# A graph attention kernel with a guarded second pass: TensorE's last branch is marked as likely taken as well

## The chip, the cores and the metric

The kernel runs on one core of a Trainium2 chip. The metric is the device time of one launch in microseconds (us). Before the change it is 612.53 us, the median of three runs (611.76, 612.53 and 612.70). One further execution was profiled.

## What is computed

Two graph attention layers (8 heads of 768 columns, then 1 head) over 512 nodes and 16,896 edges, a residual sum and a layer norm over the rows:

```python
def gat_layer(x, W, a_s, a_d, b, edge_index, concat):
    h = (x @ W).reshape(n, H, C)
    alpha_s = jnp.einsum('nhc,hc->nh', h, a_s)
    alpha_d = jnp.einsum('nhc,hc->nh', h, a_d)
    e = jax.nn.leaky_relu(alpha_s[src] + alpha_d[dst], NEG_SLOPE)
    m = jax.ops.segment_max(e, dst, num_segments=n)
    e = jnp.exp(e - m[dst])
    alpha = e / (jax.ops.segment_sum(e, dst, num_segments=n)[dst] + EPS)
    out = jax.ops.segment_sum(h[src] * alpha[:, :, None], dst, num_segments=n)
    return out.reshape(n, H * C) + b

h = jax.nn.elu(gat_layer(x, W1, ..., concat=True))
x = layernorm(x + gat_layer(h, W2, ..., concat=True))
```

## The kernel before

The edges become a dense 512x512 matrix of counts, so that each layer is a row of matrix products in float32, 128 nodes a tile. Heads are taken one after another. For each, TensorE (PE) projects x with that head's columns of W1, weighs the rows with the softmax over edges, and multiplies the result with that head's rows of W2; the sums over the heads collect in the tile `h2`. Products are split by Strassen's scheme (`P1` to `P7`, and `P0` to `P14` in thirds), which is why VectorE (DVE) adds and subtracts tiles all the time. ScalarE (ACT) takes exponentials and copies, GpSimd (POOL) issues weight loads, and SyncE (SP) issues most other transfers.

The order of the work is written by hand: strings of names such as `END`, which `run` (L724) calls one after another, so that each engine gets its instructions in the order of the names. `END` holds the last head's second half, the second layer, and the layer norm of four tiles of 128 rows. Its names that matter here:

- `f.P7.1`, `f.P5.1`, `f.P4.1`, `f.P2.1`, `f.P3.1a`, `f.P3.1b`: the last products of TensorE (L1348 and L1371);
- `all`, `inv`: mean, root and reciprocal of a tile's rows; `whole2`, `whole0`, `whole3`: the scaled rows go out in one transfer of 384 KB each, issued by SP (L1462);
- `left1`, `right1`: the last tile goes out in two halves of 192 KB, one issued by SP and one by ACT (L1455);
- `hint`: the mark that this change adds to (L1486).

A fast way of counting edges holds only where no two nodes share too many of them. So the whole pass is written twice. The first pass, with the fast count, leaves a number (`again`) which says whether it held, and behind it stands a branch on all five engines (L33): where `again` is not zero, the general pass runs, and otherwise the program goes on at a short block that stands behind the general pass. With these inputs `again` is zero, and the general pass is jumped over. Behind that block all engines meet, and the program ends.

The mark `LikelyTaken` for the branch `again` is written in `hint` for ACT, DVE and SP, near the end of `END`. As the program is built, the instruction that carries it (BRANCH_PREFETCH_HINT) doesn't stand there: on each of the three engines it is the first instruction of the first pass.

## Time and profile before

| what | value |
|---|---|
| median of the runs | 612.53 us (611.76 to 612.70) |
| the profiled execution's own time | 611.53 us |
| its span, first to last instruction | 609.7 us |
| around the span | 1.83 us |
| TensorE busy | 600.4 us, 98% of the span |
| VectorE, ScalarE, GpSimd busy | 517.9, 305.4, 100.6 us |
| bytes moved by DMA | 114.24 MB |
| granted TensorE clock | 0.997 |

Times in the views count from the span's first instruction. An engine's own name (PE for products, PEld for weight loads) stands for work of the engine, and a name that ends in q (PEldq, SPq) for its sequencer, which waits, branches and issues transfers. The page's busy times leave the sequencers out, so a branch is seen only in the view of its source line. The DMA view counts packets, bytes and, as a share of what 16 DMA engines could give in that window, the time that the packets took. Queues of the kind "instruction" bring the engines' own code.

### The profile page before, as it was taken

To read this page: it belongs to the slowest core of one execution; us is meant where nothing else is said; L and a number is where in the kernel's file an instruction comes from. 1 tells how busy PE (TensorE), PEld (TensorE's weight loads), DVE (VectorE), ACT (ScalarE), POOL (GpSimd) and SP (SyncE) were. 2 spreads that over 40 slices of the span, in tenths; PEclk is the share of its full clock that TensorE was granted. 3 is DMA by queue.
4 is the path that set the end of the run, shared out by engine and by line. 5 is a ranking of instruction groups with operands and counts; after the bars stand their busy time and mean duration, and the time that the engine had idled before them with its cause. 6 is when DMAs were issued, how large, how long until landed. Compare 5 with 4: busy or idle time off the path is not lost.

```text
span 609.7 us, 8353 instructions
## 1 busy us (share of the span) xinstructions
PE 600.4 (98%) x2812; PEld 492.3 (81%) x2812; DVE 517.9 (85%) x1027; ACT 305.4 (50%) x563; POOL 100.6 (17%) x140
## 2 busy tenths in 40 slices
PE   9999999999999999999999999999999999999994
PEld 5665685788888888888888888888888888887863
DVE  7979968779997789878897789977897789989984
ACT  3128776624745166442746066532755147744743
POOL 2210103040301302022300303012210304022001
PEclk9999999999999999999999999999999999999998
DMA  8973898794947959395955939297883949593203
GB/s 302 314 169 90 251 273 200 217 287 78 346 70 237 212 179 244 51 336 81 330 110 174 268 127 291 47 300 133 273 167 113 294 92 261 104 238 56 53 17 109
DMA packets 97343, 114.24 MB, mean 187 GB/s; under 512 B 42966, under 2 KB 78222, under 8 KB 96398
## 3 DMA queue, kind: packets, MB, share of 16 engines
q1 hardware_dynamic: 75230, 89.26, 45.9%
q0 software_dynamic: 21632, 23.79, 24.6%
q10 hardware_dynamic: 432, 0.59, 0.3%
q8 instruction: 24, 0.39, 0.3%
q14 instruction: 25, 0.20, 0.1%
HBM read 99.05 MB, written 2.90 MB: 167 GB/s over the span
## 4 chain that ended last, share of the span: by engine, by line
PE 98%; DVE 0%; ACT 0%; issue 0%; DVEq 0%
PE mm L552 22%; PE mm L472 18%; PE mm L986 17%; PE mm L413 12%; PE tr L552 5%; PE bc L986 4%; PE tr L472 4%; PE bc L472 4%; PE tr L986 3%; PE bc L552 3%; PE mm L1348 2%; PE mm L663 1%; PE bc L792 1%; PE tr L413 1%; PE bc L271 1%; PE bc L1348 0%
## 5 line engine op out<-in xcount | busy, mean ns | idle before, releaser
L560 DVE TENSOR_TENSOR h<-h,mm 128x512 f32<-128x512 f32 x74 | 50.5, 683 | 8.9 <-PE mm L552 8.1
L478 ACT ACTIVATE hs<-mm 128x512 f32<-128x512 f32 x26 | 15.5, 597 | 80.6 <-PE mm L472 79.9
L187 POOL DMA_DIRECT2D w2t<-in_L_gnn_W_dram x21 | 28.3, 1662 | 165.9 <-PE mm L472 84.0
L480 DVE TENSOR_TENSOR hs<-hs,mm 128x512 f32<-128x512 f32 x38 | 26.1, 687 | 27.0 <-PE mm L472 19.9
L986 PE MATMUL mm<-PT,hs 128*128 128x256 f32 x192 | 46.6, 380 | 0.0
L552 PE MATMUL mm<-w1r,gT 128*128 128x256 f32 x192 | 44.2, 380 | 0.0
L915 ACT ACTIVATE q<-q,rden 128x512 f32<-128x512 f32 x28 | 20.2, 720 | 42.7 <-DVE rden L899 42.5
L923 ACT COPY PT<-zr 128x1024 uint16<-128x1024 uint16 x35 | 40.4, 1158 | 2.2 <-DMA zr<-pS 1.2
L187 POOL DMA_DIRECT2D w2r<-in_L_gnn_W_dram x14 | 18.3, 1310 | 139.4 <-DVE gT L1038 77.3
L552 PEld LDWEIGHTS mm<-w1r,gT 128*128 128x128 f32 x192 | 36.4, 190 | 5.2 <-DVE gT L589 0.3
L986 PEld LDWEIGHTS mm<-PT,hs 128*128 128x128 f32 x192 | 36.2, 190 | 5.2 <-ACT u L997 0.2
L703 ACT ACTIVATE q<-q,nmax 128x512 f32<-128x512 f32 x36 | 26.0, 722 | 25.9 <-DVE nmax L700 25.9
L472 PE MATMUL mm<-w2r,gT 128*128 128x256 f32 x144 | 33.7, 379 | 0.0
L422 DVE SCALAR_TENSOR_TENSOR scr<-hs,a_s 128x768 bf16<-128x768 f32 x32 | 30.6, 955 | 0.7
L422 DVE SCALAR_TENSOR_TENSOR scr<-hs,a_d 128x768 bf16<-128x768 f32 x32 | 30.5, 952 | 0.3
L472 PEld LDWEIGHTS mm<-w2r,gT 128*128 128x128 f32 x144 | 27.3, 190 | 3.8 <-issue 0.2
L552 PE MATMUL mm<-w1t,gS 128*128 128x256 f32 x128 | 30.2, 379 | 0.0
L472 PE MATMUL mm<-w2r,xT 128*128 128x256 f32 x128 | 29.9, 379 | 0.0
L986 PE MATMUL mm<-pS,gS 128*128 128x256 f32 x120 | 29.3, 379 | 0.0
L918 ACT COPY pS<-q 128x1024 uint16<-128x1024 uint16 x27 | 28.1, 1045 | 0.7
L472 PEld LDWEIGHTS mm<-w2r,xT 128*128 128x128 f32 x128 | 24.3, 190 | 3.3
L552 PEld LDWEIGHTS mm<-w1t,gS 128*128 128x128 f32 x128 | 24.3, 190 | 3.3
(393 smaller groups left out, 1493.2 us busy)
## 6 DMA issues: line engine op xcount, KB each, us to landing
w2r<-in_L_gnn_W_dram SPq DMA_DIRECT2D x48, 384.0 KB
w1r<-in_L_gnn_W_dram SPq DMA_DIRECT2D x43, 384.0 KB
gT<-xd SPq DMA_DIRECT2D x6, 1280.0 KB
w2t<-in_L_gnn_W_dram SPq DMA_DIRECT2D x21, 256.0 KB
w2t<-in_L_gnn_W_dram POOLq DMA_DIRECT2D x21, 256.0 KB, 9.3
w1t<-in_L_gnn_W_dram SPq DMA_DIRECT2D x18, 256.0 KB
w1t<-in_L_gnn_W_dram POOLq DMA_DIRECT2D x18, 256.0 KB, 5.1
w2r<-in_L_gnn_W_dram POOLq DMA_DIRECT2D x14, 256.0 KB, 8.7
```

The source lines that it names most:

```text
L187: return lambda: nc.gpsimd.dma_start(o, part(k, n), accum_op=add)
L413: nc.tensor.matmul(ps[:, :HALF], A_[p][:, k, i * P:(i + 1) * P], B_[p][:, k, :], start=start and k == 0, stop=k == HK - 1, skip_group_chec ...
L422: return [lambda al=al, a=a, sign=sign: nc.vector.scalar_tensor_tensor(scr, HS[h][:, t, :], sign, a, op0=ALU.mult, op1=ALU.mult, accum_out ...
L472: nc.tensor.matmul(bank[chain][:, i * TH:(i + 1) * TH], A_[p][:, k, i * P:(i + 1) * P], B_[p][:, k, :], start=first and i == k == 0, stop= ...
L480: nc.vector.tensor_tensor(out(o), out(o), ps, op=how)
L552: nc.tensor.matmul(bank[chain][:, i * TH:(i + 1) * TH], A_[p][:, k, i * P:(i + 1) * P], B_[p][:, k, :], start=first and i == k == 0, stop= ...
L560: nc.vector.tensor_tensor(out(o), out(o), ps, op=how)
L703: nc.scalar.activation(q, q, AF.Exp, bias=nmax, scale=-1.0, accum_out=dens[t])
L915: nc.scalar.activation(q, q, AF.Copy, scale=rden)
L918: nc.scalar.copy(apart.rearrange("p (h n) -> p h n", h=2), q.bitcast(U16).rearrange("p (n h) -> p h n", h=2))
L923: copy(PT.rearrange("p s n -> p (s n)").bitcast(U16).rearrange("p (s n h) -> p s n h", s=NT, h=2)[:, :, t * P:(t + 1) * P, :], parted.pop( ...
L986: nc.tensor.matmul(st[bank][:, :HN], A_[p][:, k, c * P:(c + 1) * P], B_[p][:, k, :], start=start and k == 0, stop=k == 1, skip_group_check ...
```

## The change

`hint` keeps its three engines. A second step, `hintT`, writes the same mark for TensorE, and the name stands in `END` ahead of the last six calls that give TensorE work (twelve matmul statements).

```diff
-        f.fork1 f.P7.0 a3 c3 f.P6.1 zw0 f.P4.0 y22.0 sq2 sF0 f.P3.0 zu1 bn2L sA1 all2 f.P7.1 bn0L bn0R inv2 whole2 all0 f.P5.1
+        f.fork1 f.P7.0 a3 c3 f.P6.1 zw0 f.P4.0 y22.0 sq2 sF0 f.P3.0 zu1 bn2L sA1 all2 hintT f.P7.1 bn0L bn0R inv2 whole2 all0 f.P5.1
...
+    def hint_tensor():
+        if not general:
+            tc.mark_branch_hint_location("again", "LikelyTaken", [mybir.EngineType.PE])
+    ops["hintT"] = hint_tensor
```

What stands on TensorE at the start of the program, as a difference (a row with + is of the changed kernel; `zeros` is a tile that the first, empty products read; L1514 and L1519 are one and the same line of the two files):

```order
-L1514 UNCONDITIONAL_BRANCH
+L1519 UNCONDITIONAL_BRANCH
+L1519 BRANCH_PREFETCH_HINT
 L271 LDWEIGHTS zeros
 L271 MATMUL bc<-zeros 128x512
```

The one added instruction stands here, ahead of TensorE's first weight load, not where `END` names it.

What stands on TensorE in the changed kernel from the place where `END` has `hintT` to the branch (`xT`, `h` and `pS`, `PT` are the second layer's two factors, `mm`, `tr` and `bc` banks of sums):

```order
L1348 MATMUL mm_95<-h_633,PT 128x384 x2
L1348 MATMUL tr<-xT,pS 128x384 x2
L1348 MATMUL mm_95<-xT,PT 128x384 x2
L1348 MATMUL bc<-h_633,PT 128x384 x2
L1371 MATMUL tr<-h_633,pS 128x192 x4
L33 COMPARE_AND_BRANCH
```

These are the rows of before, word for word; nothing was added or moved here. The other four engines have the same instructions in the same order as before.

## The prediction

> **What bounds the kernel now.** I read the page first, for the engine that fills the span, then the last part of the chain that ended last, then the two source lines that hold the branch and the end of the program, and last the DMA view of the final microseconds, in ever narrower windows. The page:

> ```profile
> span 609.7 us, 8353 instructions
> PE 600.4 (98%) x2812; PEld 492.3 (81%) x2812; DVE 517.9 (85%) x1027; ACT 305.4 (50%) x563; POOL 100.6 (17%) x140
> PE 98%; DVE 0%; ACT 0%; issue 0%; DVEq 0%
> ```

> TensorE is busy for 98% of the span and is 98% of the chain. So a stall of TensorE ahead of its last product would lengthen the time by its full length, and only what comes behind that product is open to a change at the branch. The end of the chain, from the same view cut to the last 27 us (start, length, engine and line):

> ```profile
> 600.42 1.31 PE tr L1371 x8
> ...
> 602.69 0.30 ACT rstd L1435
> ...
> 603.41 0.67 ACT hs L1448
> ```

> TensorE's last product ends at 600.42 + 1.31 = 601.73, and the last computation of any engine at 603.41 + 0.67 = 604.08. The span goes on to 609.7: 5.6 us in which nobody computes. The branch (L33), by engine, with duration in ns (least, middle, most) and the first and last start:

> ```profile
> L33 SPq EVENT_SEMAPHORE  x8: 17/17/17, 604.9 to 607.9; - x8
> ...
> L33 PEldq COMPARE_BRANCH  x1: 3982/3982/3982, 599.3 to 599.3; - x1
> L33 POOLq COMPARE_BRANCH  x1: 45/45/45, 601.2 to 601.2; - x1
> L33 DVEq COMPARE_BRANCH  x1: 89/89/89, 603.2 to 603.2; - x1
> L33 PEldq EVENT_SEMAPHORE  x1: 51/51/51, 603.3 to 603.3; - x1
> ...
> L33 SPq COMPARE_BRANCH  x1: 73/73/73, 604.4 to 604.4; - x1
> L33 ACTq COMPARE_BRANCH  x1: 68/68/68, 604.5 to 604.5; - x1
> ```

> The reader is to see one number: 3982 ns on TensorE, against 68 to 89 ns on the three engines that carry the mark. TensorE's sequencer runs ahead of its products: it branches at 599.3, while products run until 601.73, and goes on at 603.3. The end of the program, from the line that holds it:

> ```profile
> L1514 SPq DRAIN  x3: 7/7/13, 608.8 to 609.1; - x3
> L1514 PEldq DRAIN  x2: 8/8/8, 603.5 to 609.1; - x2
> ...
> L1514 PEldq EVENT_SEMAPHORE  x2: 51/51/51, 609.0 to 609.6; - x2
> L1514 ACTq BRANCH_PREFETCH_HINT  x1: 50/50/50, 0.7 to 0.7; - x1
> L1514 SPq BRANCH_PREFETCH_HINT  x1: 51/51/51, 0.7 to 0.7; - x1
> L1514 DVEq BRANCH_PREFETCH_HINT  x1: 51/51/51, 0.8 to 0.8; - x1
> ```

> TensorE has drained at 603.5 and then waits until 609.0 for the meeting of all engines. SP comes there last: it passes eight semaphores, the last at 607.9, a dozen more behind them, and drains at 608.8. What SP waits for are the output transfers. So **the end is set by the landing of the last output, not by any branch**, and TensorE's long branch has 608.8 - 603.5 = 5.3 us to spare.

> **The change, part by part.** It adds one instruction to TensorE, the mark, at the program's start, and moves none; no queue is issued to at another place.

> The mark itself: 50 or 51 ns by the three rows above. Its neighbours on TensorE:

> ```profile
> L1505 PEldq EVENT_SEMAPHORE  x1: 51/51/51, 0.7 to 0.7; - x1
> ...
> 0.95 0.27 DVE L266 MEMSET zeros<- 128x256 uint32 x1 [0.95 <-PEq L1505]
> ...
> 1.27 0.13 PEld L271 LDWEIGHTS <-zeros 128*128 128x128 bf16 x2 [1.27 <-DVE zeros L266]
> ```

> The sequencer passes the first meeting at 0.7 and its first weight load waits until 1.27 for a tile that VectorE fills from 0.95 on. 0.05 us lie inside these 0.5 us: I take **nothing**, and 0.05 us if the cover is gone.

> The branch: by the three marked engines it should fall from 3982 ns to some 70 or 90. TensorE's sequencer would go on at about 599.4, wait for its products (601.73), drain near 602 in place of 603.5, and wait for the meeting all the same. The 3.9 us lie wholly in the 5.3 us of slack: **nothing** by itself. What is late next is what was late before, SP.

> The code packets: this is the only way to the end that I find. Two queues bring code, by the page in packets of 16 KB (0.39 MB in 24) and of 8 KB; behind them the two windows of the DMA view in which q8 moves something near the end, 600.2 to 600.4 and 604.0 to 604.2:

> ```profile
> q8 instruction: 24, 0.39, 0.3%
> q14 instruction: 25, 0.20, 0.1%
> ...
> q8 instruction: 1, 0.02, 44.6%
> ...
> q8 instruction: 1, 0.02, 39.9%
> ```

> I read q8 as TensorE's: one packet starts about 1 us behind its branch (599.3), the next when it has gone on (603.3). The first took 44.6% of 16 engines times 0.2 us = 1.43 us of one engine, the second 39.9% x 16 x 0.2 = 1.28 us. The second falls into the last wave of output transfers, issued here:

> ```profile
> 603.99 0.33 SPq L1455 DMA_DIRECT2D out_dram<-hs  x1
> 604.11 0.36 ACTq L1455 DMA_DIRECT2D out_dram<-hs  x1
> ```

> A DMA engine that spends 1.28 us on code is that much late with its sixteenth of the output. Is one engine late? Three more windows, 606.2 to 607.6, 607.1 to 607.6, and 607.135 to 607.6; q10 carries ACT's half tile, 144 packets in all by the first row (window 602 to 610), so 9 an engine:

> ```profile
> q10 hardware_dynamic: 144, 0.20, 7.1%
> ...
> DMA packets 50, 0.07 MB, mean 49 GB/s; under 512 B 7, under 2 KB 48, under 8 KB 50
> ...
> q10 hardware_dynamic: 27, 0.04, 7.1%
> q1 hardware_dynamic: 23, 0.03, 6.7%
> ...
> DMA packets 9, 0.01 MB, mean 18 GB/s; under 512 B 3, under 2 KB 9, under 8 KB 9
> ...
> DMA  3000030000300003000030000030000000000000
> DMA packets 7, 0.01 MB, mean 20 GB/s; under 512 B 1, under 2 KB 7, under 8 KB 7
> ...
> q10 hardware_dynamic: 7, 0.01, 5.4%
> ```

> Behind 606.2 there are 27 packets of q10 left: three engines with 9 each, while thirteen are done. Behind 607.1 nine are left, three of them small (an engine's closing one), behind 607.135 seven with one small: two of the three late engines close between 607.1 and 607.135. The row of digits shows what remains: packets at equal steps, about 60 ns apart (five steps in 26 slices of 11.6 ns), one engine alone. It is late by 5.4% x 16 x 0.465 = **0.40 us** against the other two, and its last packet leaves at 607.5; SP passes its last semaphore 0.4 us later, at 607.9. I take the engine that brought the 16 KB as that last one: 1.28 us of code is the largest disturbance in this stretch.

> [...] Then the two engines that are late already set the end, 0.40 us sooner. This term isn't shown by itself, so its bounds: 0, if the last engine is late for another reason or the fetch lands in the wave again; 1.28 us, the whole packet, in executions where the other two engines are not late. I take 0.40, since all three engines stand in the rows.

> [...]

> The sum: 0 + 0 - 0.40. On the profiled execution's own time, 609.7 + 1.83 = 611.53 us, that gives 611.1. The median of the runs lies 1.0 us above it; **612.53 - 0.4 = 612.1 us**.

> **The rivals.** First, **hidden anyway**: the branch gets short and the end stays, because SP waits for another transfer, or because the mark has no effect on TensorE. For it: 5.3 us of slack, and POOL, which has no mark, also branches in 45 ns, so a short branch row alone proves little. Against it: one engine is late by the size of a code packet. Time: 612.5. [...]

> [...]

> Third, **the whole packet**: in executions in which the other two engines aren't late, it costs its whole 1.28 us, and the time without it is 611.3, which is 0.21% and just faster by the bound.

> **How the numbers follow.** 0.2% is 1.2 us here, about what a measurement of this kernel can tell from no change. The forecast (-0.40) has 0.60, hidden anyway 0.30, the taken prefetch 0.05, the whole packet 0.05. Forecast and first rival are within 0.2%; of the third a little over half is beyond. So faster 0.03, same 0.92, slower 0.05. The range reaches from 612.53 - 1.28 = 611.2 (the upper bound of the one unknown term) to 612.70 + 0.05 = 612.8 (the highest run before, with the mark uncovered). It leaves out the taken prefetch, 0.05, and some scatter.

> **What would show it.** On TensorE, a mark of 50 ns at 0.7 to 0.8 us and a branch below 0.1 us at 599.3; its first drain near 602. In the DMA view, no q8 packet between 603.9 and 605.2, and one between 600 and 602.5. SP's last semaphore of the branch's line at 607.5 in place of 607.9, and a span of 609.3. If the packet is gone and SP still passes at 607.9, my reading of the late engine was wrong. If the branch still takes 4 us, the mark did nothing. [...]

## The result and the profile after

| | before | changed |
|---|---|---|
| median of 14 runs each | 611.83 us (611.07 to 612.70) | 611.02 us (610.61 to 611.71) |
| ratio to before, 95% interval | | 0.9984 (0.9977 to 0.9991) |
| profiled execution, its span | 611.53, 609.7 us | 611.11, 609.3 us |

The changed kernel is faster by 0.81 us between the medians; the interval of the ratio stands for 0.55 to 1.4 us. The forecast was 0.4 us and 612.1 us, with a range from 611.2 us on.

The changed kernel's page (the span, the engines, and the queue with the 16 KB packets):

```profile
span 609.3 us, 8354 instructions
PE 600.8 (99%) x2812; PEld 492.7 (81%) x2812; DVE 518.1 (85%) x1027; ACT 305.3 (50%) x563; POOL 100.6 (17%) x140
...
q8 instruction: 23, 0.38, 0.2%
```

One instruction more, and 23 code packets in place of 24. The branch's line and the line at the program's end:

```profile
L33 SPq EVENT_SEMAPHORE  x8: 17/17/17, 605.3 to 607.6; - x8
...
L33 PEldq COMPARE_BRANCH  x1: 393/393/393, 599.6 to 599.6; - x1
...
L33 PEldq EVENT_SEMAPHORE  x1: 51/51/51, 602.1 to 602.1; - x1
...
L1519 SPq DRAIN  x3: 7/7/13, 608.4 to 608.7; - x3
L1519 PEldq DRAIN  x2: 8/8/8, 602.2 to 608.8; - x2
...
L1519 PEldq BRANCH_PREFETCH_HINT  x1: 50/50/50, 0.8 to 0.8; - x1
```

TensorE reads its mark at 0.8 us, the branch takes 393 ns in place of 3982, and TensorE has drained at 602.2 in place of 603.5. It waits for the meeting as before, now 6.5 us (602.2 to 608.7, where its next row of that line starts). SP passes its last semaphore at 607.6 in place of 607.9.

These views count from the span's start, and the two spans are not in step: in this profile the last computation starts 0.34 us later than before (603.75 in place of 603.41). From here on I count from ACT's last issue, which is at 604.11 in the kernel before and here at

```profile
603.75 0.67 ACT L1448 ACTIVATE hs<-tr,off,rstd 128x384 f32<-128x384 f32 x1 [0.42 <-DVE off L1442]
604.33 0.33 SPq L1455 DMA_DIRECT2D out_dram<-hs  x1
604.45 0.36 ACTq L1455 DMA_DIRECT2D out_dram<-hs  x1
```

So counted, SP's last semaphore comes at 3.15 us in place of 3.83, and the span ends at 4.86 in place of 5.54: **0.68 us** less. That the span reads 609.3 us, just as forecast, is luck: the end came 0.68 us earlier, not 0.40, and the last computation happened to start 0.34 us later in this execution. In the DMA view of the changed kernel, three windows: 600.6 to 600.8, then 603 to 609, then from 2.1 us behind ACT's issue on (606.55 to 608.55), the stretch that began at 606.2 in the kernel before:

```profile
q8 instruction: 1, 0.02, 44.2%
...
q1 hardware_dynamic: 291, 0.60, 27.5%
q10 hardware_dynamic: 144, 0.20, 9.5%
q14 instruction: 4, 0.03, 1.3%
...
DMA packets 19, 0.02 MB, mean 12 GB/s; under 512 B 3, under 2 KB 19, under 8 KB 19
...
q10 hardware_dynamic: 17, 0.02, 3.1%
q1 hardware_dynamic: 2, 0.00, 0.2%
```

TensorE's next code packet is at 600.7, and the windows behind 603 have none of q8 any more. At 2.1 us 17 of ACT's output packets are left in place of 27: two late engines, not three, and these two are further on as well (2 packets of q1 left in place of 23 for three engines).

### The profile page after: what moved, and what is told of

Read it like the earlier page. It is cut to its first block, busy times and chain, and to the rows that moved or that the text cites. A ratio compares the mean times of both kernels' runs of the same rounds, so it can differ in the third digit from the quotient of the medians.

```text
span 609.3 us, 8354 instructions
## 1 busy us (share of the span) xinstructions
PE 600.8 (99%) x2812; PEld 492.7 (81%) x2812; DVE 518.1 (85%) x1027; ACT 305.3 (50%) x563; POOL 100.6 (17%) x140
## 4 chain that ended last, share of the span: by engine, by line
PE 99%; DVE 0%; ACT 0%; issue 0%; DVEq 0%
PE mm L552 22%; PE mm L472 18%; PE mm L986 17%; PE mm L413 12%; PE tr L552 5%; PE bc L986 4%; PE tr L472 4%; PE bc L472 4%; PE tr L986 3%; PE bc L552 3%; PE mm L1348 2%; PE mm L663 1%; PE bc L792 1%; PE tr L413 1%; PE bc L271 1%; PE bc L1348 0%
```

## The experiments

The run e0_after is the changed kernel again; each of the others edits it. One table gives what the packet records of each profile show, in us from ACT's last issue: the start of the 16 KB packet (the last of q8), of the 8 KB packets up to 1.1 us, the end of the closing packets of q10 behind 2.1 us (one an engine), SP's last semaphore and the span's end.

| run | 16 KB | 8 KB | late closings | SP | end | ratio to before (95%) |
|---|---|---|---|---|---|---|
| before | -0.03 | 1.00, 1.04 | 3.02, 3.02, 3.40 | 3.83 | 5.54 | |
| changed | -3.76 | 1.00, 1.05 | 2.56, 2.69 | 3.15 | 4.86 | 0.9984 (0.9977 to 0.9991) |
| e0_after | -3.76 | 1.01, 1.03 | 2.61, 2.67 | 3.12 | 4.83 | 0.9989 (0.9980 to 0.9998) |
| e1_pad2 | -2.54 | 0.85, 1.04 | 2.55, 2.68 | 3.13 | 4.84 | 0.9983 (0.9974 to 0.9992) |
| e2_pad6 | -2.43 | 0.98, 1.04 | 2.52, 2.68 | 3.13 | 4.84 | 0.9986 (0.9977 to 0.9995) |
| e3_pool | -3.77 | 1.04 | 2.67 | 3.13 | 4.82 | 0.9983 (0.9974 to 0.9992) |
| e5_late_mean | -0.25 | 0.99, 1.03 | 3.51, 3.54, 3.92 | 4.37 | 6.08 | 1.0004 (0.9995 to 1.0013) |
| e6_late_off | 0.96 | 1.01, 1.03 | 3.27, 3.76, 3.79 | 4.25 | 5.96 | 1.0001 (0.9992 to 1.0010) |
| e4_pe_only | -3.77 | 0.77, 1.03 | 2.48, 2.66 | 4.16 | 5.87 | 0.9994 (0.9985 to 1.0003) |
| e7_dve_late | -3.29 | none | none | 2.80 | 4.50 | 0.9975 (0.9966 to 0.9984) |
| e8_alone | -0.22 | none | 3.46 | 3.91 | 5.60 | 0.9999 (0.9990 to 1.0009) |
| e9_no_pe_mark | -0.17 | none | 3.08 | 3.50 | 5.20 | 0.9999 (0.9990 to 1.0008) |

The packet records don't name the DMA engine. Which packet made which engine late is read from what happens when a packet is taken away.

The theory: what the mark brings is the place of TensorE's 16 KB code packet against the last wave of outputs. The rival: the short branch itself, or the time at which TensorE is done.

**e0_after**, the changed kernel again.

> The changed kernel once more, as the reference for the other runs on this chip. Packet theory: with the mark TensorE's second code packet leaves the last wave of output transfers, and the time falls by 0.4 to 1.3 us against before (ratio 0.9979 to 0.9993); in the profile no q8 packet starts behind 603, and SP passes its last semaphore about 3.0 us after ACT's last issue in place of 3.8 (by the profiles of before and of the change). Rival (a matter of chance): ratio 1.000 within 0.0005.

Median 611.39 us against 612.12, ratio 0.9989. The profile shows the same end as the first (4.83). The gain holds on a second set of runs.

**e1_pad2 and e2_pad6**, more products behind TensorE's last:

```diff
+    def pad():
+        for _ in range(2):
+            nc.tensor.matmul(part("F", 0), A2["P3"][:, 0, P:2 * P], C2["P3"][:, 0, :], start=True, stop=True,
+                             skip_group_check=True)
...
+ ... f.P3.1b pad whole3 ...
```

> The changed kernel with 2 more float32 products of 128x384 on TensorE behind its last one (0.65 us each by the rows of L1348; nobody reads them). TensorE's branch comes 1.3 us later, its code packet starts at 602.0 in place of 600.7 and is over by 603.4, ahead of the last wave of outputs, which starts near 604.1. Packet theory: the time is that of the changed kernel within 0.3 us. Rival (it matters when TensorE is done): a third of what 6 products cost.

> The changed kernel with 6 more such products behind the last one (nobody reads them): TensorE's branch comes 3.9 us later, still short (about 0.4 us), and TensorE drains near 606, well ahead of the meeting at 608.6. Its code packet starts near 604.6, in the last wave of outputs, as in the kernel before. Packet theory: the gain is given back, the time is 0.5 to 1.0 us over the changed kernel's and within 0.3 us of before. Rival (the gain comes from the short branch itself): the time stays that of the changed kernel.

With two, 611.24 us, as expected; the packet moved by 1.2 us, the branch by only 0.3 (-4.81 to -4.49). With six, 611.38 us and an end at 4.84: the gain was not given back. But the run didn't do what it was to do. From the timeline and the branch's line of e2_pad6:

```profile
602.42 4.03 PE L1486 MATMUL mm<-h,pS 128*128 128x384 f32 x12
...
L33 PEldq COMPARE_BRANCH  x1: 388/388/388, 601.5 to 601.5; - x1
...
L33 PEldq EVENT_SEMAPHORE  x1: 51/51/51, 606.5 to 606.5; - x1
```

TensorE computes until 606.45 and branches at 601.5, 5 us ahead of its own end. Six products moved the branch by 1.3 us against ACT's issue (-4.81 to -3.51), not 3.9, and the packet never reached the wave. What the run does show: counted from ACT's last issue, TensorE may be done 3.9 us later (1.47, from 606.45 and 604.98, against -2.40, from 602.05 and 604.45) at no cost. That rules out the rival on TensorE's end, and leaves the packet open.

**e5_late_mean and e6_late_off** hold the branch by a wait, with one small product that reads a value of DVE's:

```diff
+    def late():
+        nc.tensor.matmul(part("F", 0)[:1, :2], mv[1][:, 0:1], mv[1][:, 0:2], start=True, stop=True, skip_group_check=True)
+    ops["late"] = late
...
+ ... bn1Rb all1 late hint inv1 ...
```

e6_late_off reads `off[1]` in place of `mv[1][:, 0:1]` and stands behind `inv1`.

> The changed kernel with one product of 1x2 on TensorE behind its last one that reads the last tile's mean (DVE, L1433, ready 1.4 us ahead of ACT's last issue; nobody reads the product). The 6 extra products moved the branch by only 1.3 us, since the sequencer runs ahead of them; a wait stops it. The branch stays short (about 0.4 us) but comes at -1.4 us, counted from ACT's last issue, and the 16 KB code packet at about -0.3, at the front edge of the last wave of outputs (in the kernel before: -0.03). Packet theory: the end from ACT's last issue on goes from 4.84 back to 5.3 to 5.6 us, and the time is 0.4 to 0.8 us over the changed kernel's. Rival (the short branch itself brings the gain): 4.84 stays and so does the time.

> As the run before, but the small product reads the last tile's scaled mean (DVE, L1442, ready 0.7 us ahead of ACT's last issue), so the branch comes at -0.7 and the 16 KB packet at about +0.4 us, inside the wave. Packet theory: the end from ACT's last issue on is 5.3 to 5.6 us, 0.4 to 0.8 us over the changed kernel's. Rival (the short branch itself): 4.84 us as in the changed kernel.

Both take the whole gain away: 612.40 and 612.24 us against 612.20 before. From e5_late_mean: the small product, the branch's line, the window 604.5 to 604.6 of the DMA view and the window from 606.88 (2.1 us) on:

```profile
603.47 0.19 PE L1485 MATMUL mm<-mv 128*1 128x2 f32 x2 [1.08 <-DVE mv L1433]
...
L33 SPq EVENT_SEMAPHORE  x8: 17/17/17, 605.6 to 609.2; - x8
...
L33 PEldq COMPARE_BRANCH  x1: 388/388/388, 603.5 to 603.5; - x1
...
q8 instruction: 1, 0.02, 115.6%
...
q1 hardware_dynamic: 28, 0.05, 6.9%
q10 hardware_dynamic: 27, 0.04, 4.9%
```

The branch is as short as in the changed kernel, 388 ns; only its place differs. The packet takes 115.6% x 16 x 0.1 = 1.85 us of an engine, and all 27 packets of three engines are left at 2.1 us, as before the change. So the gain is the packet's place. The size was not as expected: the ends are 6.08 and 5.96 in place of 5.3 to 5.6, and by the ratios the time is 0.7 to 1.2 us over the two runs of the changed kernel, not 0.4 to 0.8. The closings say where that comes from: the packet in the wave adds a third late engine, and the two that are late anyway (2.56 and 2.69) become later too, by 0.7 to 1.2 us, whichever of the three closings is the packet's own.

**e3_pool**: the mark for GpSimd as well.

```diff
-            tc.mark_branch_hint_location("again", "LikelyTaken", [mybir.EngineType.PE])
+            tc.mark_branch_hint_location("again", "LikelyTaken", [mybir.EngineType.PE, mybir.EngineType.Pool])
```

> The changed kernel with the mark for GpSimd as well. Packet theory: GpSimd's next 8 KB code packet (0.31 us) leaves the last wave too, so q14 moves three packets behind 605 in place of four; two engines are late for q14 packets and close within 0.13 us of each other, so one freed engine brings 0 to 0.15 us, both 0.3 us. Rival (GpSimd waits for SP's semaphore at 604.3 anyway, so its packet comes at the same time): no change, four packets.

Three 8 KB packets behind 605 in place of four, one late engine fewer, and no gain (611.43 us): the other one still closes at 2.67. So one of the two late engines was late for GpSimd's packet: with that packet, the closing at 2.56 went.

**e7_dve_late**: e3_pool, and DVE branches only when ACT is done:

```diff
+    def rest():
+        nc.vector.tensor_copy(small.tile([P, 1], F32, name="rest"), y[0][:, 1, D - 1:D])
+    ops["rest"] = rest
...
+ ... left1 right1 rest
```

> The changed kernel with the mark for GpSimd too (one late engine fewer), and one more copy of 128x1 on DVE behind its last operation that waits for ACT's last one (nobody reads it): DVE's branch comes 0.9 us later, and its 8 KB code packet at about +2.0 in place of +1.04 us from ACT's last issue, when nearly all outputs are through. Packet theory: no engine is late any more, the last closing comes at about 2.1 in place of 2.67 us, and the time is 0.4 to 0.6 us under the changed kernel's (ratio to before 0.997 to 0.998). Rival (the late engine isn't late for DVE's packet): the last closing stays at 2.6 to 2.7 and the time is the changed kernel's.

610.70 us, ratio 0.9975 (0.9966 to 0.9984): the fastest kernel of the study, 1.5 us under before. Its interval overlaps those of the changed kernel, so the step beyond that kernel rests on the profile. DVE's late branch without GpSimd's mark was not run. Its branch's line, and the DMA view from 607.04 (2.1 us) on:

```profile
L33 SPq EVENT_SEMAPHORE  x8: 17/17/17, 605.8 to 607.7; - x8
...
L33 DVEq COMPARE_BRANCH  x1: 89/89/89, 605.0 to 605.0; - x1
...
DMA packets 0, 0.00 MB, mean 0 GB/s; under 512 B 0, under 2 KB 0, under 8 KB 0
```

No packet is left at 2.1 us. The last semaphore came at 2.80, not at the 2.5 that a closing at 2.09 plus the usual 0.45 gives: three of the sixteen completions arrive 0.3 us late, beside the three code packets that now start at 2.00 to 2.09. So the end moved by 0.34 us in the profile, a little less than expected.

**e8_alone and e9_no_pe_mark**: with the 8 KB packets gone, the 16 KB packet is put back into the wave, once by the wait of e5_late_mean, once by leaving out TensorE's mark. Both edits are shown against e7_dve_late:

```diff
+ ... bn1Rb all1 late hint inv1 ...
```

```diff
-            tc.mark_branch_hint_location("again", "LikelyTaken", [mybir.EngineType.PE, mybir.EngineType.Pool])
+            tc.mark_branch_hint_location("again", "LikelyTaken", [mybir.EngineType.Pool])
```

> The kernel with DVE's late branch and GpSimd's mark, which left no 8 KB code packet ahead of +2.0 us in the last wave, and in it the small product that holds TensorE's branch until the last tile's mean is ready (nobody reads it): the 16 KB packet alone at about -0.3 us. Theory 1 (a code packet delays only the engine that carries it): one engine closes at 3.3 to 3.6 us from ACT's last issue, the other fifteen by 2.1; the time is about 1.0 us over the kernel with DVE's late branch. Theory 2 (one packet makes several engines late): three engines close behind 2.5 us, as with the mean alone (3.51, 3.54, 3.92), and the time is 1.3 to 1.6 us over it.

> The kernel with DVE's late branch and GpSimd's mark, but without TensorE's mark: the long branch is back and its second 16 KB packet at about 0.0 us in the last wave, with no 8 KB packet beside it ahead of +2.0. Theory 1 (a code packet delays only its own engine): one engine closes at 3.3 to 3.5, fifteen by 2.1, and TensorE's mark is worth 0.8 to 1.1 us here. Theory 2 (several engines): three close behind 2.5, and the mark is worth 0.8 to 1.1 us as well; the closings tell them apart. Rival (TensorE's mark brings nothing once the other packets are gone): within 0.3 us of the kernel with DVE's late branch.

611.71 and 612.03 us against 611.92 before: by the ratios the whole gain of e7_dve_late is gone both times. By the profiles the end comes 1.10 and 0.70 us later than there, so that e9_no_pe_mark ends 0.34 us ahead of the kernel before. From e8_alone, the window from 606.42 (2.1 us) on:

```profile
DMA packets 22, 0.03 MB, mean 17 GB/s; under 512 B 3, under 2 KB 19, under 8 KB 22
...
q1 hardware_dynamic: 13, 0.02, 2.8%
q10 hardware_dynamic: 9, 0.01, 1.7%
```

Nine packets of q10: one engine's share. Alone, the 16 KB packet delays its own engine (3.46, 3.08) and no other. Theory 1 holds by the closings; that of e9_no_pe_mark is earlier than the expected 3.3 to 3.5. The times alone would not decide: by the ratios both runs are 1.5 us over e7_dve_late, which for e8_alone is what theory 2 expected, and each interval reaches some 0.55 us to either side. And GpSimd's mark with DVE's late branch brings nothing where TensorE's packet is in the wave: the latest engine decides.

**e4_pe_only**: the step `hint` writes no mark, so TensorE alone has one.

```diff
-            tc.mark_branch_hint_location("again", "LikelyTaken", [mybir.EngineType.Activation, mybir.EngineType.DVE, mybir.EngineType.SP])
+            pass
```

> The changed kernel with the mark on TensorE alone, none on ACT, DVE and SP. What a mark is worth where the slack is small: SP branches at 604.7 and passes its last semaphore at 607.6. If a miss costs SP what it cost TensorE (4.0 us), SP goes on at 608.7, works off its semaphores and the time is 1.3 to 2.2 us over the changed kernel's; if it costs 2.6 us (the gap that GpSimd without a mark shows behind its branch), 0.3 to 1.0 us over. Rival (these marks are as hidden as TensorE's): within 0.3 us of the changed kernel.

611.68 us, ratio 0.9994 (0.9985 to 1.0003): about half of the gain is lost, some 0.3 to 0.6 us by the ratios of the two runs of the changed kernel, which is the lower part of the second expectation; the intervals overlap, so the loss is not shown by the times. In its profile SP passes its last semaphore at 4.16 and the span ends at 5.87, 1.0 us later than in the changed kernel, though the last output closes as early (2.66). The branch's line:

```profile
L33 SPq EVENT_SEMAPHORE  x8: 17/17/17, 608.2 to 608.7; - x8
...
L33 DVEq COMPARE_BRANCH  x1: 76/76/76, 603.7 to 603.7; - x1
L33 SPq COMPARE_BRANCH  x1: 53/53/53, 604.8 to 604.8; - x1
L33 ACTq COMPARE_BRANCH  x1: 54/54/54, 605.0 to 605.0; - x1
...
L33 DVEq EVENT_SEMAPHORE  x1: 21/21/21, 607.4 to 607.4; - x1
L33 ACTq EVENT_SEMAPHORE  x1: 17/17/17, 608.1 to 608.1; - x1
```

The same rows of the changed kernel, with marks:

```profile
L33 DVEq COMPARE_BRANCH  x1: 89/89/89, 603.6 to 603.6; - x1
...
L33 DVEq EVENT_SEMAPHORE  x1: 21/21/21, 604.3 to 604.3; - x1
...
L33 ACTq COMPARE_BRANCH  x1: 68/68/68, 604.8 to 604.8; - x1
L33 ACTq EVENT_SEMAPHORE  x1: 17/17/17, 605.3 to 605.3; - x1
```

Without marks these three branches read 53 to 76 ns, even less than with them. What the missing marks cost stands behind the row: the next instruction comes 3.1 to 3.7 us later (605.0 to 608.1 on ACT, 603.7 to 607.4 on DVE), in place of 0.5 to 0.8.

## Why the prediction was wrong

- **The time.** The start was too high: 612.53 us was the median of three runs, that of fourteen is 611.83. The forecast gain of 0.4 us from there gives 611.4; measured were 611.02. The range's lower end was set from 612.53 too, without the scatter of the runs below it, and so just missed.
- **The mark itself at nothing:** right. It stands at 0.8 us, as the built order showed, ahead of the wait for `zeros`.
- **The branch's 3.9 us inside the slack:** right. TensorE drains 1.3 us sooner and waits; e2_pad6 shows that its products could end 3.9 us later. The branch took 393 ns, not 70 to 90; nothing hangs on it.
- **The code packet as the only way to the end:** right, and shown by e5_late_mean and e6_late_off, which keep the short branch, put the packet back and lose the gain.
- **The size:** wrong. The step that failed is "the two engines that are late already set the end, 0.40 us sooner". It took them as they stood in the trace of before, as if TensorE's packet didn't touch them. It did: without it they close at 2.56 and 2.69 in place of 3.02. The end moved by 0.68 us by the profile, about 0.4 of it from the last engine (3.40 to 3.02) and 0.3 from the other two (3.02 to 2.69). No run shows the term of 0.40 us by itself, and that the packet would leave the wave was the author's estimate; the runs show that it starts 3.76 us ahead of ACT's last issue in place of 0.03, and the end 0.68 us earlier.
- **Hidden anyway** fell with the ratio's interval (0.9977 to 0.9991), and the slower case, which had 0.05, with the profile: TensorE's row has no gap of 4 us (it is busy for 600.8 us of the span, before for 600.4). The branch took 393 ns in place of 3982, with 23 code packets in place of 24. Both kernels had fetched 22 by 580 us, and behind the branch came two before and one after; which packet held the target, the records don't tell, and how the mark shortens the branch is not shown. The rows of 68 to 89 ns on the three engines that had the mark before, from which the prediction took its 70 to 90, don't show what a mark brings: without marks, in e4_pe_only, they read 53 to 76 ns, and only the gap behind them differs (3.1 to 3.7 us in place of 0.5 to 0.8).
- **The whole packet** was near the size where no other engine is late: in e8_alone and e9_no_pe_mark packets of 1.46 and 0.93 us move the last closing by 1.37 and 0.99 us against e7_dve_late (2.09), and the end by 1.10 and 0.70.

Two things stay open. Why the two engines with 8 KB packets get later when another carries 16 KB at the same time isn't explained: alone, the 16 KB packet doesn't spread. And an 8 KB packet, 0.31 us long, costs its engine more than that: 2.67 in e3_pool against 2.04 for the next closing, 0.6 us; no run looked into it.

## What to carry to other kernels

When all computing is over and the last outputs set the end, look for whatever else the DMA engines carry in those microseconds: here code packets, which came some 1 to 2 us behind the short branch of TensorE and of DVE. Here TensorE's branch was off the path and yet cost time by when its packet came: held back in e5_late_mean, it moved the end from 4.86 to 6.08 us behind ACT's last issue. The mark moved that packet (-0.03 to -3.76), the moment of the branch did too (-0.25 in e5_late_mean), and without the 8 KB packets the end came at 4.50 in place of 4.86 us (e7_dve_late) with the 16 KB packet out of the wave, while with it in the wave the time was that of before (ratio 0.9999 in e8_alone and in e9_no_pe_mark).
